# Two stacked recurrent layers on one core: the second layer's input product by Strassen on two levels as well

## The chip, the cores and the metric

The kernel runs on one core of a Trainium2 chip. The time is device time in microseconds. The kernel before took 1686.3 us (median of three runs, 1686.29 to 1686.43).

## What is computed

The input `x` holds 128 sequences of 128 time steps with 512 features, all in float32. Layer 0 is a gated recurrence, layer 1 a plain one, each with a residual connection:

```python
# layer 0, Wh and Wz are the halves of W
gate  = sigmoid(h @ Wh.T + z_t @ Wz.T + b0)
h_new = tanh(h * (1 - alpha) + gate * z_t)
x     = x + hs                       # all steps
# layer 1, on the new x
h_new = tanh(x_t @ Wx + b1 + h @ Wh1)
out   = x + hs
```

Both layers start from the same condition tensor (128 x 512). The products with `h` (the state products) must be made step by step. The products with the inputs (`z @ Wz.T`, `x @ Wx`) can be made for several steps at once.

## The kernel before, in words

**Tiling.** A step's activations lie transposed in SBUF, features on the partitions, as 4 blocks of 128 features by 128 sequences. Steps are taken in groups of `G` = 4; `ring[g]` (tile `T`) holds a group's inputs, and the residuals are added into it. Layer 1 runs `LAG` = 9 steps behind layer 0, so in most steps `t` TensorE makes layer 0's state product of step t, layer 1's of step t - 9, and a share of the input products.

**State products.** Each is 2 halves of 8 matmuls of 128 x 128 x 128 (`state_product`, L332) into the PSUM tiles `r0a`, `r1a` (layer 0) and `r0b`, `r1b` (layer 1). Those tiles are seeded beforehand with the input product: layer 1's by a copy on ScalarE (`seed`, L328), layer 0's by one VectorE addition of two terms (`seed_deep`, L474). Then follow, for layer 0 on each half, the sigmoid on ScalarE (`gate0`, L522), three VectorE operations (`mix0`, L528 and L531), the tanh (`tanh0`, L536), and for layer 1 one tanh (`tanh1`, L551). GpSimd adds each half to the residual (L540).

**Input products.** For a group of 4 steps, the matrix product is split into 2 x 2 blocks and made by Strassen's scheme in 7 products, in the order `OUTER` = 1, 2, 6, 5, 7, 3, 4. Layer 1 (`multiply`, L268) makes each of the 7 by 4 matmuls with 256 columns. Layer 0 (`multiply_deep`, L403) splits each of the 7 again, into 7 matmuls with 128 columns. The activations that Strassen's scheme needs beside the plain blocks are sums: the outer ones (tiles `sa`, `sb`, 512 wide, four per group) are made on GpSimd, layer 0's inner ones (tile `inner`, raw and nested, eight operations of 512) on VectorE, all at L210.

The products of a group accumulate into PSUM: 1, 6, 7 and 4 into one set, 5 and 3 into another, 2 into a third (layer 1) or again the second (layer 0). Between the products of one set the running sum has to be read out. After 1, 6 and 5 ScalarE copies it to SBUF (`keep`, L277; `keep_deep`, L416), after 2, 7 and 3 VectorE adds it to an earlier copy (`add`, L294; `add_deep`, L437), after 4 ScalarE copies it (`last`). A set of layer 0 is two PSUM banks, moved by two operations of 512 and 384 elements. For layer 0 two more VectorE operations on half a group join the inner parts (`gather`, L471 and L472).

**Order.** All operations are put at planned times (`at(time, fn, ...)`) and emitted sorted by time; each engine's queue then runs strictly in that order, and only semaphores make it wait. A step's start is the sum of planned costs: `STATE` for a state product, `PRODUCT` for one of the 7 products of the plain kind, `DEEP` for one of the twice split kind. The shares of a period of four steps are: in the first, layer 1's products 7, 3, 4; in the second, layer 0's 1, 2, 6, 5; in the third, layer 0's 7, 3, 4; in the fourth, layer 1's 1, 2, 6, 5. Steps with 3 and with 4 products thus alternate. In the last group and after it (t >= 125) layer 1 runs with fewer products per step, and at the end alone.

Of the kernel before, what the change touches and what calls it, by code (L numbers as in the profile page):

```python
# [13 lines left out]
def kernel(  # L14
# [37 lines left out]
    P = 128  # L52
# [17 lines left out]
    work = ctx.enter_context(tc.tile_pool(name="work", bufs=2))  # L70
# [8 lines left out]
    STATE, PRODUCT, DEEP = 3.57, 1.73, 1.56  # L79
    OUTER = 1, 2, 6, 5, 7, 3, 4  # L80
# [24 lines left out]
    for t in range(T + LAG + 4):  # L105
        start.append(clock)
        layers = (t < T) + (t >= LAG)
        busy = STATE * layers + (STATE + 0.6 if t < G - 1 else 0.0)
        for layer, g, which in shares(t):
            busy += (DEEP if layer == 0 and g > 1 else PRODUCT) * len(which)  # L110
        clock += max(busy, STATE + (3.0 if t < T else 0.7))
# [39 lines left out]
    cond_in = work.tile([P, C, P], F32, tag="s", name="cond_in")  # L151
    condT = const.tile([P, C, P], F32, tag="condT", name="condT")

    def load_small():
        nc.gpsimd.memset(rows, 0.0)
        for i, v in enumerate((b0, alpha, b1)):
            nc.gpsimd.dma_start(
                out=rows[: Q * C, i], in_=v.rearrange("(a j) -> a j", j=S)
            )
        cond_view = cond.rearrange("(a i) (q r) -> q i a r", i=S, q=Q)  # L160
        for q in range(Q):
            nc.gpsimd.dma_start(out=cond_in[q * S : (q + 1) * S], in_=cond_view[q])

# [36 lines left out]
    COMBINATION = {5: 0, 6: 1, 7: 2, 4: 3}  # L200

    def sums(eng, out, a, which):
# [3 lines left out]
            6: (lambda: out(0), lambda: a(0, 0), ALU.subtract),  # L206
            7: (lambda: a(0, 0), lambda: a(1, 0), ALU.subtract),
            3: (lambda: a(0, 1), lambda: out(1), ALU.subtract),
        }[which]
        eng.tensor_tensor(out(SUM[which]), one(), two(), op)  # L210
# [11 lines left out]
    banks = {}  # L222

    def bank(tag, name):
        banks[tag] = psum.tile([P, 4, P], F32, tag=tag, name=f"{tag}_{name}")

    class Layer:

        X, V, V2 = "B0", "B1", "A1"

        def __init__(self, name):
            self.name = name
            self.S, self.kept, self.pre, self.state = {}, {}, {}, {}
            self.w = const.tile([P, C, C, P], F32, tag=f"w{name}", name=f"w{name}")
            self.wh = const.tile([P, C, C, P], F32, tag=f"wh{name}", name=f"wh{name}")
            self.wc = const.tile([P, 4, 2, 2, P], F32, tag=f"wc{name}", name=f"wc{name}")

# [5 lines left out]

        def act(self, g, i, k):
# [3 lines left out]
        def add_up(self, g, which):  # L248
            if which == 5:
                self.S[g] = spool.tile(  # L250
                    [P, 4, 2, H, P], F32, tag=f"s{self.name}", name=f"s{self.name}_{g}"
                )
            sums(nc.gpsimd, lambda j: self.S[g][:, j], lambda i, k: self.act(g, i, k), which)

        def left(self, g, i):
            return self.S[g][:, SUM[i]] if i in SUM else self.act(g, *PAIRS["left"][i])

        def right(self, i):
            return self.wc[:, COMBINATION[i]] if i in COMBINATION else self.block(*PAIRS["right"][i])

        def multiply(self, g, i, tag, first):
            if first:
                bank(tag, f"{self.name}_{g}_{i}")
            ps = banks[tag].rearrange("p (m h) b -> p m (h b)", m=2)
            a, w = self.left(g, i), self.right(i)
            for m in range(2):
                for c in range(2):
                    nc.tensor.matmul(  # L268
                        ps[:, m], w[:, c, m, :], a[:, c],
                        start=first and m == 0 and c == 0, stop=c == 1, skip_group_check=True,  # L270
                    )

        def evacuate(self, dst, tag, half):

            for m in range(2):
                f = 2 * half + m
                nc.scalar.activation(  # L277
                    dst[:, 2 * m : 2 * m + 2], banks[tag][:, 2 * m : 2 * m + 2], AF.Identity,
                    bias=per_feature[:, 2, f : f + 1],
                )  # L280

        def keep(self, g, i, tag, half):
            s = spool.tile([P, 4, P], F32, tag=f"k{self.name}_{i}", name=f"k{self.name}_{g}_{i}")
            self.evacuate(s, tag, half)
            self.kept[i] = s

        def result(self, g, i, half):
            self.pre[g, i, half] = cpool.tile(
                [P, 4, P], F32, tag=f"c{self.name}_{i}{half}", name=f"c{self.name}_{g}_{i}{half}"
            )  # L290
            return self.pre[g, i, half]

        def add(self, g, i, half, tag, kept):
            nc.vector.tensor_tensor(self.result(g, i, half), banks[tag], self.kept[kept], ALU.add)  # L294

        def last(self, g, tag):
            self.evacuate(self.result(g, 1, 0), tag, 0)

        def products(self, g, which, time):

            X, V, V2 = self.X, self.V, self.V2
            plan_of = {
                1: (X, True, self.keep, (g, "p1", X, 0)),
                5: (V, True, self.keep, (g, "p5", V, 1)),
                6: (X, False, self.keep, (g, "u2", X, 1)),
                3: (V, False, self.add, (g, 0, 1, V, "u2")),
                7: (X, False, self.add, (g, 1, 1, X, "p5")),
                2: (V2, True, self.add, (g, 0, 0, V2, "p1")),
                4: (X, False, self.last, (g, X)),
            }  # L310
            for i in which:
                tag, first, fn, args = plan_of[i]
                at(time, self.multiply, g, i, tag, first)
                time += PRODUCT
# [3 lines left out]
        def from_inputs(self, t, half):  # L318
            g, k = divmod(t, G)
            return self.pre[g, k // H, half][:, k % H :: H]  # L320
# [7 lines left out]
        def seed(self, t, half):  # L328

            nc.scalar.copy(self.state_bank(t, half), self.from_inputs(t, half))  # L330
# [10 lines left out]

    INNER = 1, 2, 6, 3, 7, 4, 5

    class DeepLayer(Layer):

        X, V, V2 = "A0", "B0", "B0"

        def __init__(self, name):
            super().__init__(name)
            self.wi = const.tile([P, 2, 4, 4, P], F32, tag=f"wi{name}", name=f"wi{name}")  # L350
            self.inner, self.parts = {}, {}

        def combine_inner(self, kind, which, eng):

            out = self.wi[:, kind]
            if kind == 0:
                w = self.w.rearrange("p (k a) (n b) f -> p a b k n f", a=2, b=2)
                out = out.rearrange("p (k n) j f -> p j k n f", k=2)
                combinations(eng, lambda j: out[:, j], lambda a, b: w[:, a, b], which)
            else:  # L360
                combinations(eng, lambda j: out[:, :, j], lambda a, b: self.wc[:, :, a, b], which)

        def add_up_inner(self, g, kind, which, eng):
            if kind == 0 and which == 5:
                self.inner[g] = spool.tile([P, 2, 4, 4, P], F32, tag="inner", name=f"inner_{g}")
            out = self.inner[g][:, kind]
            if kind == 0:
                x = ring[g].rearrange("p (k a) (i b) n -> p b a i k n", a=2, b=2)
                out = out.rearrange("p (i k) j n -> p j i k n", i=2)
                sums(eng, lambda j: out[:, j], lambda b, a: x[:, b, a], which)  # L370
            else:
                sums(eng, lambda j: out[:, :, j], lambda b, a: self.S[g][:, :, a, b], which)

        def left_inner(self, g, outer, i):
            if outer in SUM:
# [321 lines left out]
```

## Time and profile before

| | before |
|---|---|
| median of 3 runs | 1686.3 us |
| the profiled execution | 1686.1 us |
| its span | 1684.3 us (1.8 us lie around it) |
| granted TensorE clock | 0.999 |
| busy: TensorE, VectorE, ScalarE, GpSimd | 1662.6, 1036.1, 687.8, 798.3 us |
| one period of four steps | 51.62 us |

The span is what the profile's times count from. "PE" is TensorE, "PEld" its weight loads, "DVE" VectorE, "ACT" ScalarE, "POOL" GpSimd, "SP" the queue that issues most DMAs. A matmul in float32 stands as two records, so 4 matmuls are "x8" and 7 are "x14". A matmul's recorded end lies some 0.16 us behind the start of the next one, as they are pipelined; the time that a matmul costs is therefore read from start to start. One core runs, so there is one row of everything.

The period is read off the starts of layer 1's products: 407.77 and 459.39 us, and so on through the span.

### The profile page before, as it was taken

Reading aid. Unit: us, or ns where it says so; the run is one execution under the profiler, and the core shown is the slowest. Engines: PE = TensorE matmul, PEld = TensorE weight load, DVE = VectorE, ACT = ScalarE, POOL = GpSimd, SP = SyncE. Lnnn points to the kernel's source line nnn. Section 1 sums busy time; section 2 is a strip of 40 time slices with the busy share of each in tenths; the row PEclk is TensorE's granted clock in tenths of the full one; section 3 lists DMA queues with packets and bytes.
Section 4 is the critical chain, followed back from the end, with each engine's and each line's share of the span. In section 5 each row is a group of like instructions: output and inputs, shape, how many; then the busy total and the mean of one; then the engine's idle time right before and its main releaser. Section 6 shows DMA issues by size and latency. Waiting matters only on the chain.

```text
span 1684.3 us, 33340 instructions
## 1 busy us (share of the span) xinstructions
PE 1662.6 (99%) x13108; PEld 1611.2 (96%) x13108; DVE 1036.1 (62%) x1924; ACT 687.8 (41%) x1796; POOL 798.3 (47%) x788
## 2 busy tenths in 40 slices
PE   6999999999999999999999999999999999999998
PEld 6999999999999999999999999999999999999998
DVE  4676666666566665666666666656666666666431
ACT  1544344444344433444434444344444344444343
POOL 3754445544444554355444445543554444554333
PEclk9999999999999999999999999999999999999999
DMA  8101211121121112111211111112111111110112
GB/s 173 53 14 41 46 41 39 40 50 39 39 46 44 39 39 45 44 39 39 48 42 39 43 42 43 38 42 48 38 39 44 45 39 38 44 46 20 20 32 51
DMA packets 153212, 73.76 MB, mean 44 GB/s; under 512 B 16800, under 2 KB 151968, under 8 KB 153056
## 3 DMA queue, kind: packets, MB, share of 16 engines
q1 hardware_dynamic: 148992, 69.53, 18.5%
q10 hardware_dynamic: 3840, 1.84, 0.6%
q8 instruction: 103, 1.69, 0.4%
q14 instruction: 53, 0.43, 0.1%
q0 software_dynamic: 224, 0.27, 0.1%
HBM read 38.02 MB, written 33.55 MB: 42 GB/s over the span
## 4 chain that ended last, share of the span: by engine, by line
PE 95%; DMA 2%; DVE 1%; ACT 1%; issue 0%; SPq 0%; POOLq 0%; POOL 0%; DVEq 0%; ACTq 0%
PE B_b L268 20%; PE r0b L337 14%; PE r1b L337 13%; PE r0a L337 13%; PE r1a L337 13%; PE A_a L403 11%; PE B_a L403 8%; PE A_b L268 3%; DMA x<-in_x_dram 1%; DVE s L531 0%; DMA wh_in<-in_L_cond_W_dram 0%; DMA wz_in<-in_L_cond_W_dram 0%; PE r1a L493 0%; SPq L122 0%; PE B_a L268 0%
## 5 line engine op out<-in xcount | busy, mean ns | idle before, releaser
L540 POOL TENSOR_TENSOR T<-T,h 128x256 f32<-128x256 f32 x512 | 429.8, 851 | 758.5 <-ACT h L536 726.0
L337 PE MATMUL r0a<-h,wha 128*128 128x128 f32 x2032 | 248.5, 275 | 1.1 <-ACT h L536 1.1
L337 PE MATMUL r0b<-h,whb 128*128 128x128 f32 x2032 | 248.4, 275 | 0.1
L337 PE MATMUL r1b<-h,whb 128*128 128x128 f32 x2032 | 247.7, 275 | 0.0
L337 PE MATMUL r1a<-h,wha 128*128 128x128 f32 x2032 | 247.6, 275 | 0.0
L337 PEld LDWEIGHTS r0a<-h,wha 128*128 128x128 f32 x2032 | 242.2, 192 | 5.1 <-ACT h L536 1.7
L337 PEld LDWEIGHTS r0b<-h,whb 128*128 128x128 f32 x2032 | 237.8, 192 | 1.0 <-ACT h L551 0.7
L337 PEld LDWEIGHTS r1a<-h,wha 128*128 128x128 f32 x2032 | 237.1, 192 | 0.0
L337 PEld LDWEIGHTS r1b<-h,whb 128*128 128x128 f32 x2032 | 237.1, 192 | 0.0
L536 ACT ACTIVATE h<-s 128x256 f32<-128x256 f32 x256 | 106.7, 417 | 305.4 <-DVE s L531 305.4
L528 DVE TENSOR_TENSOR r0a<-r0a,T 128x256 f32<-128x256 f32 x128 | 54.9, 429 | 250.6 <-ACT r0a L522 250.6
L268 PE MATMUL B_b<-sb,wcb 128*128 128x256 f32 x768 | 176.3, 379 | 0.0
L268 PEld LDWEIGHTS B_b<-sb,wcb 128*128 128x128 f32 x768 | 143.3, 190 | 18.1
L522 ACT ACTIVATE r0a<-r0a,per_feature 128x128 f32<-128x128 f32 x256 | 87.6, 342 | 154.8 <-PE r0a L337 150.6
L210 POOL TENSOR_TENSOR sa<-T 128x512 f32<-128x512 f32 x62 | 93.0, 1500 | 119.5 <-DVE T L174 119.5
L403 PE MATMUL A_a<-inner,wia 128*128 128x128 f32 x720 | 139.2, 275 | 0.0
L179 DVE STREAM_TRANSPOSE o<-T 128x512 f32<-128x512 f32 x128 | 90.1, 704 | 36.9 <-POOL T L540 33.6
L528 DVE TENSOR_TENSOR r1a<-r1a,T 128x256 f32<-128x256 f32 x128 | 55.3, 432 | 91.0 <-ACT r1a L522 91.0
L403 PEld LDWEIGHTS A_a<-inner,wia 128*128 128x128 f32 x720 | 109.3, 192 | 0.0
L403 PE MATMUL B_a<-inner,wia 128*128 128x128 f32 x540 | 104.4, 275 | 0.0
L210 DVE TENSOR_TENSOR inner<-sa 128x512 f32<-128x512 f32 x60 | 86.0, 1434 | 23.3 <-POOL sa L210 23.3
L174 DVE STREAM_TRANSPOSE T<-x 128x512 f32<-128x512 f32 x128 | 86.8, 681 | 13.1 <-DMA x<-in_x_dram 12.1
(137 smaller groups left out, 2628.6 us busy)
## 6 DMA issues: line engine op xcount, KB each, us to landing
out_dram<-o SPq DMA_DIRECT2D x510, 64.0 KB, 1.8
x<-in_x_dram SPq DMA_DIRECT2D x502, 64.0 KB, 2.5
wx_in<-in_L_cond_Wx_dram SPq DMA_DIRECT2D x4, 256.0 KB, 7.0
wh_in<-in_L_cond_Wh_dram SPq DMA_DIRECT2D x4, 256.0 KB, 9.5
x<-in_x_dram ACTq DMA_DIRECT2D x10, 64.0 KB, 4.0
wz_in<-in_L_cond_W_dram ACTq DMA_DIRECT2D x2, 256.0 KB, 6.2
wz_in<-in_L_cond_W_dram SPq DMA_DIRECT2D x2, 256.0 KB, 5.6
wh_in<-in_L_cond_W_dram ACTq DMA_DIRECT2D x2, 256.0 KB, 6.0
```

The source lines that it names most:

```text
L174: nc.vector.transpose(dst.rearrange("p c (a i) -> p c a i", i=S), src.rearrange("p a (c j) -> p c a j", j=S))
L179: nc.vector.transpose(dst.rearrange("p a (c j) -> p c a j", j=S), src.rearrange("p c (a i) -> p c a i", i=S))
L210: eng.tensor_tensor(out(SUM[which]), one(), two(), op)
L268: nc.tensor.matmul(ps[:, m], w[:, c, m, :], a[:, c], start=first and m == 0 and c == 0, stop=c == 1, skip_group_check=True,)
L337: nc.tensor.matmul(ps[:, m], self.wh[:, c, 2 * half + m, :], h[t - 1][:, c], start=alone and m == 0 and c == 0, stop=c == C - 1, skip_grou ...
L403: nc.tensor.matmul(banks[f"{tag}{part}"][:, place], self.right_inner(outer, i), self.left_inner(g, outer, i), start=first and place == 0, ...
L522: nc.scalar.activation(gate[:, m], gate[:, m], AF.Sigmoid, bias=per_feature[:, 0, f : f + 1])
L528: nc.vector.tensor_tensor(gate, gate, at_of(t)[:, two[i]], ALU.mult)
L536: nc.scalar.activation(h0[t][:, two[i]], s0[t][:, two[i]], AF.Tanh)
L540: nc.gpsimd.tensor_tensor(r, r, h[t][:, two[i]], ALU.add)
```

## The change

Layer 1 is given the same class as layer 0. Each of its 7 products becomes 7 matmuls of 128 columns, with its own inner weight combinations (`raw`, `nested`) and inner sums of activations. Only layer 0's group 1 keeps the plain products. With that:

- **PSUM sets.** There are two sets of two banks, `A` and `B`. A set is one tile of 8 places, of which 7 are used, and is moved by one operation of 896 elements (`keep`, `add`, `last`) in place of two of 512 and 384 (layer 0) or of 512 or twice 256 (layer 1). Layer 0 accumulates 1, 6, 7, 4 in A and 2, 5, 3 in B; layer 1 the other way round.
- **Sums.** The raw sums are made for three of the four blocks only, the nested ones for two pairs; they become VectorE operations of 256 (`R12`, `N56`, `N73`) and 128 elements (`R4`), 16 per group and layer. All sums lie in tiles that both layers share by turns (`buffer`). `sum_up` lays down when they are made.
- **Seeds.** Both layers' state tiles are seeded by a ScalarE copy (`seed`) and a VectorE addition in place (`seed_second`).
- **Bias and residual.** Layer 1's bias moves from the copies to the tanh, which becomes two operations of 128 elements per half. The residual is one GpSimd operation of 512 elements in place of two of 256.
- **Times.** `finish` (the transposition and the stores of the output) and `prepare_x` move from 0.6 and 0.7 us after a step's start to 6.35 and 6.4 us. At the start, 16 matmuls on a zeroed tile are put ahead of everything (`warm_up`), and several preparations move between engines and steps.

```diff
+    def cost(layer, g):
+        return PRODUCT if (layer, g) == ("a", 1) else DEEP
...
+    def warm_up():
+        ps = [L1.state_bank(-1, half) for half in range(2)]
+        for n in range(16):
+            nc.tensor.matmul(
+                ps[n % 2].rearrange("p m b -> p (m b)"), condT[:, 0], condT[:, 0:2].rearrange("p c b -> p (c b)"),
+                start=True, stop=True,
+            )
...
+        def add_up_raw(self, g, row, which, eng):
+            x = ring[g].rearrange("p (k a) (i b) n -> p b a i k n", a=2, b=2)
+            if row == 0:
+                out = buffer((self.name, g), "R12", [P, 2, 4, P])
+                sums(eng, lambda j: out[:, :, SUM[j]], lambda b, a: x[:, b, a, 0], which)
+            else:
+                out = buffer((self.name, g), "R4", [P, 4, P])
+                sums(eng, lambda j: out[:, SUM[j]], lambda b, a: x[:, b, a, 1, 1], which)
+
+        def add_up_nested(self, g, pair, which, eng):
+            S = shared[(self.name, g), "S" + pair]
+            out = buffer((self.name, g), "N" + pair, [P, 2, 4, P])
+            sums(eng, lambda j: out[:, :, SUM[j]], lambda b, a: S[:, :, a, b], which)
...
         def multiply(self, g, outer, tag, first):
+            if first:
+                sets[tag] = psum.tile([P, 8, P], F32, tag=tag, name=f"{tag}_{self.name}_{g}_{outer}")
...
+            for n, i in enumerate(INNER):
+                nc.tensor.matmul(
+                    sets[tag][:, n], self.right(outer, i), self.left(g, outer, i),
+                    start=first and n % 4 == 0, stop=True, skip_group_check=True,
+                )
...
+        def keep(self, g, i, tag):
+            self.kept[i] = spool.tile([P, 7, P], F32, tag=f"k_{i}", name=f"k{self.name}_{g}_{i}")
+            n = self.places(g)
+            nc.scalar.copy(self.kept[i][:, n], sets[tag][:, n])
...
         def add(self, g, i, half, tag, kept):
+            n = self.places(g)
+            nc.vector.tensor_tensor(self.part(g, i, half)[:, n], sets[tag][:, n], self.kept[kept][:, n], ALU.add)
...
         def seed(self, t, half):
-            nc.scalar.copy(self.state_bank(t, half), self.from_inputs(t, half))
+            nc.scalar.copy(self.state_bank(t, half), self.terms(t, half)[0])
+
+        def seed_second(self, t, half):
+            for term in self.terms(t, half)[1:]:
+                ps = self.state[t, half]
+                nc.vector.tensor_tensor(ps, ps, term, ALU.add)
...
-    L0, L1 = DeepLayer("a"), Layer("b")
+    L0, L1 = Layer("a", "A", "B"), Layer("b", "B", "A")
...
-    def residual(t, i, h):
-        r = at_of(t)[:, two[i]]
-        nc.gpsimd.tensor_tensor(r, r, h[t][:, two[i]], ALU.add)
+    def residual(t, h):
+        nc.gpsimd.tensor_tensor(at_of(t), at_of(t), h[t], ALU.add)
...
     def tanh1(t, i):
...
-        nc.scalar.activation(h1[t][:, two[i]], ps, AF.Tanh)
+        for m in range(2):
+            f = 2 * i + m
+            nc.scalar.activation(h1[t][:, f], ps[:, m], AF.Tanh, bias=per_feature[:, 2, f : f + 1])
...
-        at(start[3] + 0.1 + 0.4 * kc, permute_w1, L1.w, "wx", kc)
+        at(start[1] + 2.5 + 0.1 * kc, permute_w1, L1.w, "wx", kc)
...
+    def sum_up(layer, g, outer, b, c):
+        for n, i in enumerate((5, 6, 3, 7)):
+            at(outer[n // 2] + 0.1 * n, layer.add_up, g, i, nc.gpsimd)
+            at(b + 0.1 + 0.01 * n, layer.add_up_raw, g, 0, i, nc.vector)
+            at(b + (3.3, 3.31, 5.1, 5.11)[n], layer.add_up_nested, g, "56", i, nc.vector)
+            at(c + 0.1 + 0.01 * n, layer.add_up_nested, g, "73", i, nc.vector)
+            at(c + (3.3, 3.31, 5.1, 5.11)[n], layer.add_up_raw, g, 1, i, nc.vector)
...
-                    at(end + 0.5 if (u + 1) % G else due, L1.seed, u + 1, i)
-                at(end + 0.6, residual, u, i, h1)
-            at(start[t + 1] + 0.6 if u + 1 < T else end + 1.4, finish, u)
+                    if (u + 1) % G:
+                        copy, add = end + 0.6, end + 1.05
+                    else:
+                        copy, add = (start[t + 1] + x if t + 1 < T else start[t + 1] - 0.02 for x in (0.05, 1.4))
+                    at(copy, L1.seed, u + 1, i)
+                    at(add, L1.seed_second, u + 1, i)
+            at(end + 0.7, residual, u, h1)
+            at(start[t + 1] + 6.35 if t + 1 < T else end + 1.4, finish, u)
...
+        if k == 1 and 0 <= g - 2 < NG:
+            at(start[t] - (0.9 if t < T else 0.03), L1.gather, g - 2, 0, nc.vector)
+            at(start[t] + 1.0 if t >= T else start[t + 1] - 0.9, L1.gather, g - 2, 1, nc.vector)
+        if k == 0 and 3 <= g + 1 < NG:
+            sum_up(L0, g + 1, (start[t] + 9.0, start[t + 1] + 9.0), start[t + 1], start[t + 2])
+        if k == 2 and 1 <= g - 1 < NG - 2:
+            sum_up(L1, g - 1, (start[t] + 9.0, start[t + 1] + 9.0), start[t + 1], start[t + 2])
```

## The prediction, made before the changed kernel ran

> **What bounds the kernel now.** First the page's busy times, then the windows (name of the stretch, its length, busy time of PE, PEld, DVE, ACT, POOL with instructions, granted clock, DMA share, GB/s):
>
> ```profile
> PE 1662.6 (99%) x13108; PEld 1611.2 (96%) x13108; DVE 1036.1 (62%) x1924; ACT 687.8 (41%) x1796; POOL 798.3 (47%) x788
> ...
> 160.00:1600.00 1440.00, 1440.00 (x11436) 1399.51 (x11435) 915.36 (x1694) 597.53 (x1561) 685.99 (x668) 1.00 0.18 41
> 1640.00:1684.00 44.00, 38.70 (x295) 36.70 (x293) 7.48 (x11) 13.82 (x36) 15.19 (x19) 0.97 0.27 54
> ```
>
> PE has no gap in 160 to 1600 us, at full clock; DVE is busy 64% of that stretch. So a shorter PE stream shortens the kernel until another engine delivers too late. The chain that ended last prices PE's pieces (start, us, what):
>
> ```profile
> 80.30 1.79 PE r1a L337 x16
> 82.09 1.56 PE A_a L403 x14
> 83.65 1.73 PE B_b L268 x8
> ```
>
> A product of layer 1 costs 1.727 us (24 records take 5.18), one of layer 0's twice split kind 1.563 (starts 419.93, 421.50, 423.06), a half state product 1.786. A period is 8 x 3.573 + 7 x 1.727 + 7 x 1.563 = 51.6 us, the period measured.
>
> Who delivers to PE in a step is read off the timeline of one that starts at S = 400.46:
>
> ```profile
> 400.46 1.95 PE L337 MATMUL r0a<-h,wha 128*128 128x128 f32 x16
> 402.45 0.72 ACT L522 ACTIVATE r0a<-r0a,per_feature 128x128 f32<-128x128 f32 x2 [0.95 <-PE r0a L337]
> 403.20 0.43 DVE L528 TENSOR_TENSOR r0a<-r0a,T 128x256 f32<-128x256 f32 x1 [3.29 <-ACT r0a L522]
> 404.36 0.42 ACT L536 ACTIVATE h<-s 128x256 f32<-128x256 f32 x1 [1.20 <-DVE s L531]
> 404.69 0.70 ACT L522 ACTIVATE r1a<-r1a,per_feature 128x128 f32<-128x128 f32 x2
> 405.42 0.43 DVE L528 TENSOR_TENSOR r1a<-r1a,T 128x256 f32<-128x256 f32 x1 [0.68 <-ACT r1a L522]
> 405.88 0.61 DVE L531 SCALAR_TENSOR_TENSOR s<-h,leak,r1a 128x128 f32<-128x128 f32 x2
> ```
>
> DVE begins the second mix at S+4.96 and ends it at S+6.03, whatever the change does in between, since it waits for ACT's second sigmoid. Last the groups by shape, for prices (busy, mean ns, idle before):
>
> ```profile
> L210 DVE TENSOR_TENSOR inner<-inner,sa 128x512 f32<-128x512 f32 x16 | 10.9, 683 | 0.0
> L210 DVE TENSOR_TENSOR inner<-T,inner 128x512 f32<-128x512 f32 x16 | 17.6, 1101 | 0.6
> L472 DVE TENSOR_TENSOR ca<-ca 128x256 f32<-128x256 f32 x30 | 18.9, 629 | 1.0
> L437 DVE TENSOR_TENSOR ca<-B_a,ka_u 128x512 f32<-128x512 f32 x15 | 10.4, 692 | 5.1 <-PE B_a L403 5.1
> L437 DVE TENSOR_TENSOR ca<-B_a,ka_u 128x384 f32<-128x384 f32 x15 | 8.4, 558 | 0.0
> ```
>
> One kind of sum takes 0.68 or 1.10 us: the long ones lie beside a running POOL operation. L472 is likewise two operations in one, 0.42 at 437.98 with POOL idle and 0.83 at 445.15 beside it. Additions that read PSUM (L437) take 0.69 in both cases.
>
> **Part 1, the products.** Each of 32 groups saves 7 x (1.727 - 1.563) = 1.15 us of PE: **-36.8**. All of it lies on the path; the new period is 50.47.
>
> **Part 2, DVE.** Prices: 256 elements 0.43, 512 0.69, 128 some 0.30 (from 0.683 and 0.425 by a straight line), 896 from PSUM 0.692 + 384 x (0.692 - 0.558)/128 = 1.09. A period of four steps then holds 8 transpositions 5.5, 8 mixes of 1.07 8.6, 16 second seeds 6.9, 6 additions 6.6, 4 gathers of 1.11 4.5, 24 sums of 256 10.3, 8 sums of 128 2.4: **44.8 us of 50.5**, against some 33.0 before (660.6 in 400 to 1432 us, 20 periods). DVE is not the bound, but its order now matters. I follow it through a period.
>
> The tightest step is the third, layer 0's 7, 3, 4. Product 4 writes into set A, so PE waits there for the addition after product 7. Queued ahead of that on DVE, after the second mix (S+6.03): two R4 sums 0.60, two transpositions 1.37, four second seeds 1.72, the addition 1.09; S+10.81. Successive independent operations overlap by 0.07 (L531 ends 406.49, a seed starts 406.52, the next operation 406.87, before the seed's end): seven times, S+10.3. PE is there at 7.15 + 2 x 1.563 = S+10.27. The fourth seed waits for ACT (last tanh, then copy, at S+8.7); it falls due at 8.75, so that wait is nearly hidden. Stall: 0.05 to 0.1.
>
> In the first step two of the seeds fall after the gather, 0.7 us of slack. Behind it, though, DVE has add, gather, four R12 sums and then layer 1's seeds: add from S+10.45, gather to S+12.9 (one operation beside POOL), R12 to S+14.6, first seed to S+15.0, which is 3.2 us into the next step; PE wants it 3.57 in. Slack 0.4. The mix behind it starts 0.7 late. In steps of four products PE needs the addition after product 2 by S+11.84; product 2 ends at S+10.44, the addition at S+11.55: 0.3. ACT's copy after product 1 (0.585 + 3 x 0.107 = 0.91 us, S+9.3 to S+10.2) must end before product 6 at S+10.27: 0.1.
>
> So every handover fits, some by 0.1 to 0.4. What can break them is a DVE sum beside POOL: +0.41 (L472) to +1.06 (a sum of 683 reached 1.75). By the order, POOL's residual comes after the second mix and its sums after the second residual, while DVE has transpositions and PSUM operations; mainly the gathers (11.5 to 12.9) meet POOL. I take **0.15 us per period, x 29 = +4.4**; between 0 and 0.84 (two handovers late by 0.42).
>
> [...]
>
> **Part 3, ACT and POOL.** ACT per period: 32 halves of gate and tanh of layer 1 at 0.35, 8 tanhs 0.42, 16 copies 0.38, 8 set copies 0.91 = 28 of 50.5, hidden. POOL: 16 operations of 1.27 = 20, hidden; before, 24.7. The stores leave 5.7 us later on SP, behind them only loads that are needed 17 us on: nothing.
>
> **Part 4, the end.** From t = 128 PE waits for layer 1 alone. The tanh as two operations ends 0.70 instead of 0.38 after PE: 4 bare steps, +1.3. Group 31 now needs gather and second seed between its additions and step 124 of layer 1: the addition after product 3 ends 0.3 before PE is done, gather 1.1, copy 0.4, second seed 0.5: +1.8 (before, the copy was done 0.37 early, 1663.08 against 1663.45). One residual of 1.27 for 0.72 at the end: +0.55. One late seed at t = 129: +0.3. Sum **+4.0**.
>
> **Part 5, the start.** PE's first matmuls run at half speed (timeline, records of four):
>
> ```profile
> 13.97 1.06 PE L493 MATMUL r0a<-T,wa 128*128 128x128 f32 x4
> 14.82 1.06 PE L493 MATMUL r1a<-T,wa 128*128 128x128 f32 x4
> 15.68 0.74 PE L493 MATMUL r0a<-T,wa 128*128 128x128 f32 x4
> ...
> 22.89 1.99 PE L268 MATMUL A_a<-sa,wca 128*128 128x256 f32 x8 [1.69 <-POOL sa L210]
> ```
>
> Four records take 0.85 at first and 0.45 from 16.2, with the page's clock at full. The warm-up should make the input product 1.9 us shorter, but two products later PE waits for POOL's sums until 22.89 all the same: 0 on the path. [...] Moved to step 1, layer 1's weight copies on ACT (2.18 us at 56.73) stand ahead of `tanh0`: +1.1; step 3 loses them, -0.3. The inner sums of group 2 left PE idle twice for 0.92 (waits for `h` at 70 and 78 us); their smaller form should return one. Taken as **0**, between -2 and +3.
>
> **Sum.** Against the profiled execution, 1686.1 (0.2 under the median): 1686.1 - 36.8 + 4.4 + 4.0 + 0 = **1657.7**, say 1658.
>
> **Rivals.**
>
> *Handovers late.* In two of four steps a POOL meeting of 0.42 lies ahead of the addition that PE waits for: 0.84 x 29 = 24.4 in place of 4.4: 1678. For it: margins of 0.1 to 0.4, and rows of 1.1 to 1.75. Against: the order puts POOL's work beside PSUM operations.
>
> *DVE becomes the bound: slower.* 40 operations per period (32 sums, 8 halves of gathers) have two SBUF inputs, before 12. At 0.42 for each that meets POOL, DVE passes the old period from (51.6 - 44.8)/0.42 = 17 on. At 24 of 40 the period is 54.9, 3.3 x 29 = 96 more: about 1786. For it: POOL is busy 40% of the time, and the late engine stays late. Against: POOL's 16 operations are fewer than before and come while DVE has other work.
>
> *No stall at all*, a tail of +2: 1686.1 - 36.8 + 2 = 1651, the low end.
>
> **Chances.** Forecast with its 0 to 0.5 us per period (1648 to 1670): 0.60. Handovers late (1670 to 1683): 0.24. Between them and no change: 0.05. DVE the bound: 0.11. A measurement here can tell 0.2%, 3.4 us. Faster 0.84, same 0.05, slower 0.11. Range 1648 to 1682: it leaves out the slow cases, and little at the low end (no stall, no tail, 2 us from the start).
>
> **What would show it.** Right: layer 1's products at 1.563 and periods of 50.5 to 50.7; the wait of PE on DVE's `add` under 5 us in total; PE near 99%. Wrong: L224 sums of 256 at a mean above 0.7 us, PE waiting for seeds (`r0b`) or for `h` each period, or a period over 51.6.

## The result, and the profile after

| | before | after |
|---|---|---|
| median | 1686.4 us (4 runs beside the changed kernel) | 1671.3 us (1667.7 to 1672.0) |
| ratio | | 0.9906, 95% interval 0.9888 to 0.9923 |
| the profiled execution, its span | 1686.1, 1684.3 us | 1672.0, 1670.2 us |
| granted TensorE clock | 0.999 | 0.994 |
| one period of four steps | 51.62 us | 50.48 us |

The changed kernel is faster, by 14 to 15 us and not by the forecast 28. The time lies in the forecast range (1648 to 1682) and its sign is right; half of the gain is missing, and the two profiles say where. First the page's busy times and the windows of the changed kernel (columns as in the prediction):

```profile
PE 1642.3 (98%) x14484; PEld 1633.5 (98%) x14484; DVE 1321.9 (79%) x2976; ACT 793.5 (48%) x2046; POOL 666.0 (40%) x541
```

```profile
0.00:26.00 26.00, 19.49 (x87) 16.29 (x88) 13.56 (x24) 1.87 (x2) 10.77 (x18) 0.93 0.87 163
26.00:40.00 14.00, 13.76 (x83) 12.26 (x83) 6.29 (x15) 4.55 (x9) 5.41 (x5) 0.89 0.74 192
...
160.00:1600.00 1440.00, 1438.38 (x12879) 1438.08 (x12878) 1177.86 (x2676) 707.31 (x1830) 571.30 (x454) 1.00 0.18 42
1600.00:1640.00 40.00, 34.49 (x287) 34.10 (x286) 22.28 (x43) 14.47 (x39) 12.76 (x10) 0.91 0.20 40
1640.00:1670.00 30.00, 21.60 (x169) 20.84 (x167) 10.13 (x18) 9.69 (x29) 6.33 (x5) 0.90 0.22 45
```

Through the long middle PE is as full as before (1438.4 of 1440 us) at full clock, though DVE went from 915 to 1178 us. Both ends have a granted clock of 0.89 to 0.93 (the kernel before had 1.00 from 26 to 40 and from 1600 to 1640 us) and, at the back, a PE that stands: 34.5 of 40 us busy. PE's longest waits name the places (us in total, times, longest):

```profile
PE r0b L435 <- DVE r0b L428: 8.1, 3, 4.8
PE A_a L343 <- POOL S_a L224: 3.3, 1, 3.3
PE B_b L349 <- DVE cb L373: 3.0, 3, 1.6
```

A ledger makes this exact. For each step the start of its state product on PE is read from the timeline, and the one of the changed kernel is subtracted from that of the kernel before: what has been gained up to there, in us of the profiled executions (u counts layer 1's steps).

| up to | after | e_first_group | e_finish | e_plain1 | e_best |
|---|---|---|---|---|---|
| layer 0, t = 0 | -2.46 | -2.52 | -0.91 | -1.31 | -0.69 |
| t = 2 | -3.31 | -2.77 | -1.76 | -2.16 | -0.93 |
| t = 6 | -2.12 | -2.47 | -0.57 | -0.97 | -0.61 |
| t = 11 | -6.01 | -4.75 | -4.44 | -0.37 | -2.03 |
| t = 13 | -4.86 | -3.60 | -3.30 | -0.37 | -0.89 |
| t = 117 | 24.68 | 25.95 | 26.25 | -0.37 | 28.66 |
| t = 124 | 26.48 | 27.74 | 28.05 | -0.37 | 30.46 |
| t = 125 | 25.08 | 26.36 | 26.65 | -0.37 | 30.79 |
| layer 1, u = 118 | 25.73 | 27.01 | 27.30 | -0.37 | 31.44 |
| u = 120 | 20.45 | 21.72 | 27.81 | -0.62 | 32.09 |
| u = 123 | 18.80 | 19.45 | 25.46 | -0.62 | 31.17 |
| u = 125 | 14.90 | 15.57 | 24.23 | -0.62 | 33.04 |
| end of the span | 14.1 | 14.8 | 23.5 | -1.4 | 32.2 |

From t = 13 to 117 the gain is 29.54 us in 26 periods, 1.136 per period against 1.15 forecast. So the products pay what was promised. Measured against the 1.15 us that each of layer 1's groups was to bring, some 7 us are lost before t = 11, 1.9 around step 124 and some 13 after layer 0's end. My theory was: the start loses to a fallen clock and to sums that come late for layer 1's first group, the end to the order on DVE. The rival: the new work on DVE is too much everywhere, and whatever is moved only changes the place of the wait.

### The profile page after: what moved, and what is told of

Same layout as the page of the kernel before. It is cut to its first block, busy times and chain, and to the rows that moved or that the text cites. A ratio compares the mean times of both kernels' runs of the same rounds, so it can differ in the third digit from the quotient of the medians.

```text
span 1670.2 us, 37100 instructions
## 1 busy us (share of the span) xinstructions
PE 1642.3 (98%) x14484; PEld 1633.5 (98%) x14484; DVE 1321.9 (79%) x2976; ACT 793.5 (48%) x2046; POOL 666.0 (40%) x541
## 4 chain that ended last, share of the span: by engine, by line
PE 90%; DVE 3%; issue 3%; POOL 2%; ACT 1%; DMA 1%; POOLq 0%; ACTq 0%; DVEq 0%; SPq 0%
PE r0a L435 13%; PE r0b L435 13%; PE r1b L435 13%; PE r1a L435 12%; PE A_a L349 11%; PE B_b L349 11%; PE A_b L349 8%; PE B_a L349 8%; POOL T L493 1%; DMA x<-in_x_dram 1%; DVE h L485 1%; PE A_a L343 0%; DVE cb L373 0%; DVE N_b L224 0%; POOL S_a L224 0%
## 5 line engine op out<-in xcount | busy, mean ns | idle before, releaser
L493 POOL TENSOR_TENSOR T<-T,h 128x512 f32<-128x512 f32 x256 | 326.6, 1276 | 973.6 <-ACT h L490 890.2
L490 ACT ACTIVATE h<-h 128x256 f32<-128x256 f32 x256 | 106.7, 417 | 276.7 <-DVE h L485 273.9
L435 PEld LDWEIGHTS r0a<-h,wha 128*128 128x128 f32 x2032 | 237.3, 192 | 0.7 <-ACT h L490 0.6
L476 ACT ACTIVATE r1a<-r1a,per_feature 128x128 f32<-128x128 f32 x256 | 85.3, 333 | 4.2
L502 ACT ACTIVATE h<-r0b,per_feature 128x128 f32<-128x128 f32 x256 | 78.1, 355 | 16.6 <-PE r0b L435 16.6
L224 POOL TENSOR_TENSOR S_a<-T 128x512 f32<-128x512 f32 x62 | 79.8, 1287 | 14.6 <-DVE T L187 14.6
L502 ACT ACTIVATE h<-r1b,per_feature 128x128 f32<-128x128 f32 x256 | 80.8, 371 | 10.1 <-PE r1b L435 8.0
L224 POOL TENSOR_TENSOR S_b<-T 128x512 f32<-128x512 f32 x64 | 81.8, 1278 | 1.5 <-issue 1.5
L485 DVE SCALAR_TENSOR_TENSOR h<-h,leak,r0a 128x128 f32<-128x128 f32 x254 | 77.0, 345 | 5.3
L485 DVE SCALAR_TENSOR_TENSOR h<-h,leak,r1a 128x128 f32<-128x128 f32 x254 | 77.1, 345 | 4.5
```

The source lines that it names most:

```text
L224: eng.tensor_tensor(out(which), one(), two(), op)
L435: nc.tensor.matmul(ps[:, m], self.wh[:, c, 2 * half + m, :], h[t - 1][:, c], start=alone and m == 0 and c == 0, stop=c == C - 1, skip_grou ...
L476: nc.scalar.activation(gate[:, m], gate[:, m], AF.Sigmoid, bias=per_feature[:, 0, f : f + 1])
L485: nc.vector.scalar_tensor_tensor(h0[t][:, f], h0[t - 1][:, f], leak[:, f : f + 1], gate[:, m], ALU.mult, ALU.add)
L490: nc.scalar.activation(h0[t][:, two[i]], h0[t][:, two[i]], AF.Tanh)
L493: nc.gpsimd.tensor_tensor(at_of(t), at_of(t), h[t], ALU.add)
```

## The start: what the warm-up did

PE's rows of the changed kernel at the start (the timeline; start, us, what, and in brackets the idle time before and who ended it):

```profile
17.87 1.89 PE L343 MATMUL B_a<-T,wa 128*128 128x256 f32 x8
23.07 3.78 PE L343 MATMUL A_a<-S_a,wca 128*128 128x256 f32 x8 [3.31 <-POOL S_a L224]
26.64 3.04 PE L343 MATMUL B_a<-S_a,wca 128*128 128x256 f32 x8
29.52 1.89 PE L343 MATMUL A_a<-S_a,wca 128*128 128x256 f32 x8
```

The warm-up did shorten the input product, from 5.5 to 4.2 us. PE then came earlier to the same wait for POOL's sums, stood 3.31 us in place of 1.69, and the two products behind the gap took 3.57 and 2.88 us instead of 2.34 and 1.83. Two runs tell the parts apart.

**Without the warm-up.** In `warm_up`, 2 products in place of 16:

```diff
-        for n in range(16):
+        for n in range(2):
```

> The changed kernel with 2 warm-up products in place of 16. Theory: the warm-up costs the start. It shortens the input product, but the sums on POOL are not earlier, so PE stands for 3.31 us before product 6 (1.69 in the kernel before), and the two products behind that gap took 3.57 and 2.88 us in place of 1.73. Without it the gap is again some 1.7 us, both products take 1.73, and layer 0's first state product starts near 30.5 us in place of 32.97: 2.5 us faster than the changed kernel's 1671.3. Rival: PE's first matmuls at half speed are on the path and the warm-up saves their 1.9 us: 1.9 us slower, first state product near 35.

Measured: 1669.3 us (0.9898, 0.9883 to 0.9912). The gap is 1.81 us, the products behind it take 2.34 and 1.83 us as in the kernel before, and layer 0 starts at 31.14 in place of 32.97 us: 1.8 better, not 2.5, since in this run PE had POOL's sums only at 23.52 us, 0.63 later than in the kernel before. The rival's 1.9 us to the other side is excluded.

**With the gap filled.** Seven products of 256 columns, used by nobody, between product 2 and product 6:

```diff
+    def fill():
+        ps = [L1.state_bank(-2, half) for half in range(2)]
+        for n in range(7):
+            nc.tensor.matmul(
+                ps[n % 2].rearrange("p m b -> p (m b)"), L0.w[:, 0, 0], L0.w[:, 0, 0:2].rearrange("p m f -> p (m f)"),
+                start=True, stop=True,
+            )
...
+    at(19.12, fill)
```

> The changed kernel with seven more products of 256 columns, whose result nobody uses, between product 2 and product 6 of layer 0's first group, where PE stands for 3.31 us. Theory: it is the standing itself that brings the granted clock down; with PE busy for about 3.0 of the 3.3 us, products 6 and 5 take 1.73 us each and the first state product starts near 30.0 to 30.5 us in place of 32.97: 2.5 to 3 us faster than the changed kernel. Rival: the granted clock falls because PE began early and has worked a fixed time; then products 6 and 5 stay at 3.6 and 2.9 us, and the time is the changed kernel's.

Measured: 1668.6 us (0.9896, 0.9881 to 0.9911). The same rows:

```profile
22.38 0.59 PE L181 MATMUL r0b_-2_227<-wa 128*128 128x256 f32 x2
22.89 1.99 PE L352 MATMUL A_a<-S_a,wca 128*128 128x256 f32 x8
25.23 1.99 PE L352 MATMUL B_a<-S_a,wca 128*128 128x256 f32 x8 [0.35 <-DVE ca L382]
```

PE has no gap, product 6 is at full speed, and layer 0 starts at 30.51 us, to 0.01 where it started before the change. Of the 2.46 us, 2.28 are the two products behind the longer standing (6.45 us against 4.17), and 0.18 that POOL's sum was ready later in the changed kernel (PE went on at 23.07, here at 22.89). Beginning early had nothing to do with it. The medians of these runs and of the next (1668.6 to 1670.4) lie within the spread of the changed kernel's own (1667.7 to 1672.0): the rows decide here, not the times.

## Layer 1's first group

**Copies and raw sums moved.** The raw sums one step earlier; ACT's copies of layer 1's weights (2.17 us, from 43.52) behind step 1's second tanh:

```diff
-        at(start[1] + 2.5 + 0.1 * kc, permute_w1, L1.w, "wx", kc)
+        at(start[1] + 5.4 + 0.1 * kc, permute_w1, L1.w, "wx", kc)
-        at(start[1] + 3.0 + n, L1.combine_weights, i, nc.gpsimd)
+        at(start[1] + 5.8 + 0.01 * n, L1.combine_weights, i, nc.gpsimd)
-        at(start[6] + (2.6, 2.61, 4.4, 4.41)[n] - 0.2, L1.add_up_raw, 0, 0, i, nc.vector)
+        at(start[5] + 0.1 + 0.01 * n, L1.add_up_raw, 0, 0, i, nc.vector)
```

> The changed kernel with two things moved at the start: the raw sums of layer 1's first group one step earlier on DVE (PE waited 1.85 us for them within that group's first product), and ACT's copies of layer 1's weights from ahead of step 1's first tanh to behind its second (with POOL's sums of these weights behind them). Theory: the changed kernel loses some 7 us in its first eleven steps, about 1.85 of it to the late raw sums and 0.85 to the copies: 2 to 2.7 us faster than the changed kernel at step 11. Rival: DVE is full there and whatever is moved makes the next thing late (additions after product 7, first seeds): under 0.7 us.

Measured: 1670.4 us (0.9905, 0.9890 to 0.9920), and by the ledger 1.26 us at t = 11, between the two. The copies gave 0.60 (t = 0 to 2). PE's wait for the raw sums is gone (1.6 us better from t = 6 to 7), but their four operations, each 0.57 to 0.95 us beside POOL, now make step 5's mix late, and 0.9 is lost there (t = 2 to 6). Here the rival is half right.

## The steady part: how near the edge it is

The prediction's narrowest handover, the addition after product 7 in the third step, in the changed kernel (timeline; this step starts at 425.34):

```profile
433.94 0.42 DVE L428 TENSOR_TENSOR r1b<-r1b,cb 128x256 f32<-128x256 f32 x1
...
434.27 1.08 DVE L373 TENSOR_TENSOR ca<-A_a,ka_p 128x896 f32<-128x896 f32 x1
...
435.61 0.50 PE L349 MATMUL A_a<-T,wca 128*128 128x128 f32 x3
```

The addition ends at 435.35 and PE goes on at 435.61 without a gap. To see whether these 0.26 us are all there is, one instruction that nobody needs was put ahead of that addition in 27 periods:

```diff
+    def extra():
+        nc.vector.tensor_tensor(spare, condT[:, 0:2], condT[:, 2:4], ALU.add)
...
+        if k == 2 and 3 <= g < NG - 2:
+            at(start[t] + 8.74, extra)
... e_extra_2: twice; e_extra_turn: in place of the sum
+        nc.vector.transpose(spare.rearrange("p c (a i) -> p c a i", i=S), condT[:, 0:2].rearrange("p c (a i) -> p c a i", i=S))
```

> The changed kernel with one sum of 256 elements more on DVE in 27 periods (0.42 us by the trace), right ahead of the addition after product 7 of layer 0, the tightest handover. Its result is not used. Theory: in the changed kernel that addition ended 0.26 us before PE needed it; 0.34 to 0.42 more leaves 0.08 to 0.16 us of PE idle, 27 times: 2 to 4.5 us more by the last step of layer 0, with PE's periods going from 50.48 to 50.6. Rival A (as forecast: no margin): 0.34 to 0.42 times 27, 9 to 11 us. Rival B (DVE has 18% of its time free and makes it good elsewhere): nothing.

> The same with two such sums in each of the 27 periods. Theory (margin 0.26): 0.42 to 0.58 us each time, 11 to 16 us more. Rival A (no margin): 18 to 23. Rival B (slack elsewhere): nothing. Between this run and the one with one sum the step is a whole sum, 0.34 to 0.42 us per period, if the margin is used up by the first.

> The changed kernel with one more DVE operation of the same size at the same place as the extra sum, but a transposition, which has one input (0.35 us, half of the 0.70 that one of 512 elements takes). Theory: the extra sum cost 0.64 us per period because it has two inputs in SBUF and took 0.81 us beside POOL's sum, not because DVE had 0.42 us more to do; a transposition there keeps its 0.35 us, of which the margin of 0.26 takes most: 0 to 0.1 us per period, 0 to 3 us in all. Rival: what counts is one more instruction in a full queue (and the restart of PE after each wait): 0.3 to 0.6 us per period, 8 to 16 us, as with the sum.

Measured: 1687.6 us with one sum (1.0002, 0.9993 to 1.0012: the whole gain of the change is gone), 1726.0 with two (1.0235, 1.0220 to 1.0251), 1673.4 with the transposition (0.9924, 0.9910 to 0.9937). No theory had the sums right. The transposition cost 0.24 us per period, between the theory (0 to 0.1) and the rival (0.3 to 0.6); its time rose by 2 us only, but not as the theory had it: part of the ledger's 6.1 us was made good by a start that lost nothing (t = 0 at +0.12, where the changed kernel lost 2.46). The mean pitches in that step, from the start of one product on PE to the next:

| | addition later by | product 3 | product 4 | PE's loss per period | t = 13 to 117 by the ledger |
|---|---|---|---|---|---|
| after | | 1.566 | 1.567 | | |
| one transposition | 0.33 | 1.704 | 1.665 | 0.24 | 6.1 |
| one sum | 0.73 | 2.109 | 1.665 | 0.64 | 16.7 |
| two sums | 2.14 | 3.516 | 1.703 | 2.1 | 54.9 |

In each row, what the addition is late by, less what product 3 grows by, is the margin: 0.19 us each time. So the margin is 0.2 (the 0.26 of the trace less some 0.06 to hand over), and each stall costs a further 0.10 to 0.14 in the product behind it (1.665 and 1.703 against 1.567). The surprise is the size of the sums. DVE and POOL in the runs with one and with two (each sum is 0.42 us elsewhere):

```profile
435.67 1.27 POOL L498 TENSOR_TENSOR T<-T,h 128x512 f32<-128x512 f32 x1 [0.37 <-ACT h L507]
...
436.41 0.81 DVE L180 TENSOR_TENSOR spare<-condT 128x256 f32<-128x256 f32 x1
...
436.90 1.46 POOL L229 TENSOR_TENSOR S_b<-T 128x512 f32<-128x512 f32 x1
...
437.14 1.08 DVE L378 TENSOR_TENSOR ca<-A_a,ka_p 128x896 f32<-128x896 f32 x1
```

```profile
442.37 1.27 POOL L498 TENSOR_TENSOR T<-T,h 128x512 f32<-128x512 f32 x1 [0.36 <-ACT h L507]
...
443.11 2.22 DVE L180 TENSOR_TENSOR spare<-condT 128x256 f32<-128x256 f32 x2
...
443.60 1.45 POOL L229 TENSOR_TENSOR S_b<-T 128x512 f32<-128x512 f32 x1
```

The one sum comes while POOL's residual runs and ends at 437.22, 0.28 after that ends at 436.94. POOL's next sum, issued meanwhile, takes 1.46 in place of 1.27. With two, the second sum ends at 445.33, again 0.28 after POOL's sum ends at 445.05. In these rows the two engines take turns, instruction by instruction. The transposition, with one input, took 0.43 us in all 27 places; the one at 432.83 ran while POOL was at a residual (432.10 to 433.37).

## The second level undone

Layer 1 by one level again (`e_plain1`): every place that names layer 0's group 1 as plain now names layer 1 too, and layer 1's raw and nested sums, its nested weights and its gathers go.

```diff
-            if (self.name, g) == ("a", 1):
+            if (self.name == "b" or g == 1):
```

> The changed kernel with layer 1's products by Strassen on one level again (8 matmuls of 256 columns in place of 14 records of 128), without layer 1's inner sums and gathers; warm-up, sets of two banks and shared tiles stay. Theory: the second level is worth its full 1.15 us in each of layer 1's 32 groups while PE is the bound, and costs what was lost in the first layer-1 group (some 3.5 us in steps 7 to 10), in step 124 (1.9) and in the last ten steps (some 12): so the period is again 51.62, and the time lands near 1671.3 + 36.8 - 17 = 1691, with 2.5 to 3.3 us of the loss at the start still there: slower than the kernel before by 2 to 6 us. Rival: the losses at the end come from the other parts (sets of two banks, the tanh in two operations) and stay: 1700 to 1708.

Measured: 1687.4 us (1.0007, 0.9997 to 1.0016). The period is the old one to the last digit (the ledger stands at -0.37 from t = 9 to 127), DVE is at 829 us in the window from 160 to 1600, the start loses 0.4 us and the end 1.0. So everything else in the change (sets of two banks, shared tiles, the tanh in two operations, one residual operation) costs 1.4 us in all, and what is lost from t = 6 to 11, at t = 124 and behind layer 0's end comes with layer 1's second level: its sums, gathers and second seeds. It came out 4 us lower than expected, mostly because the start lost 0.4 us and not 2.5 to 3.3.

## The end: one instruction that waits at the head of a queue

DVE, PE and POOL in the changed kernel where PE stands longest (timeline):

```profile
1612.73 1.26 POOL L493 TENSOR_TENSOR T<-T,h 128x512 f32<-128x512 f32 x1 [5.33 <-ACT h L502]
...
1614.02 0.71 DVE L192 STREAM_TRANSPOSE o<-T 128x512 f32<-128x512 f32 x1 [4.12 <-POOL T L493]
1614.66 0.83 DVE L224 TENSOR_TENSOR N_b<-S_b,N_b 128x256 f32<-128x256 f32 x1
1615.41 1.75 DVE L402 TENSOR_TENSOR cb<-cb 128x512 f32<-128x512 f32 x1
...
1617.87 0.42 DVE L428 TENSOR_TENSOR r0b<-r0b,cb 128x256 f32<-128x256 f32 x1
...
1618.35 3.79 PE L435 MATMUL r0b<-h,whb 128*128 128x128 f32 x16 [4.80 <-DVE r0b L428]
```

From t = 127 on `finish` is planned 1.4 us behind the step's second half, before POOL has done that step's residual. DVE stands 4.12 us at its transposition, with the gather and the seeds that PE needs behind it; the gather then meets POOL's sums and takes 1.75 us for 0.69. PE stands 4.80 us, and its next half product takes 3.58 us for 1.79. The same happens at u = 124 (2.32 us, then 3.52).

**The transposition moved**, and with it (in the run named e_tail) group 30's gather ahead of the sums. In e_tail the last step's transposition came ahead of its residual, so that addition is not in that kernel's last step and its end is some 2.2 us shorter than e_finish's (by the ledger from u = 127 on); its time is too good by that much.

```diff
-            at(start[t + 1] + 6.35 if t + 1 < T else end + 1.4, finish, u)
+            at(start[t + 1] + 6.35 if t + 1 < T else start[t + 1] + 2.0 if u + 1 < T else end + 1.4, finish, u)
... e_tail only:
-            at(start[t] - (0.9 if t < T else 0.03), L1.gather, g - 2, 0, nc.vector)
+            at(start[T] + 0.2 if t == T + 1 else start[t] - (0.9 if t < T else 0.03), L1.gather, g - 2, 0, nc.vector)
```

> The changed kernel with another order on DVE in the last ten steps: the transposition of a finished step stands behind the next additions and seeds (it waits 3 to 4 us for POOL's residual), and group 30's gather ahead of the sums that wait for POOL. Theory: of the 25.7 us gained by step 127, some 11 are lost behind it in two waits of PE for a seed (4.80 and 2.32 us) and in the low clock after each (2.3 and 1.7 us). The 4.8 us wait goes with its low clock, the 2.3 us one shrinks to about 1.5: 8 to 10 us faster than the changed kernel, about 1662. Rival: what bounds these steps is the chain of tanh, additions, gather and seeds that each step needs (longer since the change), and the order in DVE's queue hardly matters: under 2 us.

> The changed kernel with one move: from the end of layer 0 on, DVE's transposition of a finished step stands some 2 us into the next step, behind that step's additions, gather and seeds (the last step keeps its place). The gather of group 30 stays where it was. Theory: this instruction, which waits 3 to 4 us for POOL's residual with everything else of DVE's queue behind it, makes about half of what the tail loses; the rest is the gather that meets POOL, which stays: 4 to 7 us faster than the changed kernel, PE's longest wait for a seed (4.80 us) down to 1 to 3. Rival: the wait for POOL only fills time in which DVE has nothing to do; the late sums and gather make the loss: under 1.5 us.

Measured: e_tail 1662.3 us (0.9855, 0.9839 to 0.9871), e_finish 1663.8 us (0.9867, 0.9852 to 0.9882). From u = 119 to 127 the changed kernel loses 10.4 us, e_finish 3.6: 6.8 won, and the step from u = 119 to 120 loses nothing. The gather's move adds nothing to that (e_tail loses 5.2 there). The rival falls.

## All of it together

`e_best` takes the filler, the two moves at the start, and further: the nested sums of layer 1's first group in one go, its block of raw sums for product 4 ahead of step 8's second mix, its first seeds between the next group's raw sums; the nested sums for step 126 planned in step 125, not 124, and the sums behind them a step later too; the last steps' transpositions 3.0 us into the next step; their gathers where both inputs are ready (the first 0.2 us into a step); and the last group's products as below.

```diff
-(OUTER[0:1], OUTER[1:2], OUTER[2:3], OUTER[3:5], OUTER[5:])
+(OUTER[0:1], OUTER[1:2], OUTER[2:4], OUTER[4:6], OUTER[6:])
...
-                    if (u + 1) % G:
+                    if (u + 1) % G or t >= T:
...
-        at(start[7] + (2.6, 2.61, 4.4, 4.41)[n], L1.add_up_nested, 0, "56", i, nc.vector)
+        at(start[7] + 2.6 + 0.01 * n, L1.add_up_nested, 0, "56", i, nc.vector)
...
-                at(start[t + 1] + 1.4, L1.seed_second, 0, i)
+                at(start[t + 1] + 0.115, L1.seed_second, 0, i)
```

> The changed kernel with its losses taken one by one: seven products nobody uses in PE's gap at the start; layer 1's weight copies behind step 1's second tanh; raw and inner sums of layer 1's first group earlier, its first seeds ahead of half of the next group's raw sums; inner sums for step 126 spread over steps 124 and 125; the last steps with the transpositions of finished steps behind the seeds, gathers where both inputs are ready, and the last group's products as 1, 1, 2, 2, 1 per step in place of 1, 1, 1, 2, 2. Theory: the ledger of the changed kernel adds up, so the losses come back: about 2 us from the clock, 3 to 4 from the other items at the start, 1.5 to 1.9 in step 124, 8 to 10 in the last ten steps: 1654 to 1657, some 30 us under the kernel before. Rival: part of them are one chain seen twice, and what is moved makes the next thing late: 1659 to 1664, no better than the run with the transposition alone moved.

Measured: **1653.7 us** (1653.3 to 1653.9; ratio to the kernel before 0.9807, 0.9794 to 0.9820), 17.5 us under the changed kernel's median and 10 under e_finish: the low edge of the theory (1654 to 1657), far from the rival (1659 to 1664). In its window from 1600 to 1640 us PE has no gap:

```profile
1600.00:1640.00 40.00, 40.00 (x355) 39.75 (x354) 27.88 (x49) 18.54 (x47) 13.65 (x11) 1.00 0.22 43
```

By the ledger the steps from u = 118 to 127 now win 1.6 us where the changed kernel lost 10.9, step 124 wins 0.3 where it lost 1.4, and t = 0 to 11 loses 1.3 where it lost 3.6. Which of the further moves gave how much within these stretches was not told apart.

## Why the prediction was right, and where it was not

The sign and the steady part were foreseen. That the time lies in the range is partly luck: 1671.3 us lies above the forecast's own stretch (1648 to 1670, chance 0.60) and in that of the rival "Handovers late" (1670 to 1683, 0.24), whose 0.84 us per period did not come. Losses of 22.3 us at the start, in step 124 and at the end, which the sum had at 4.0, put it there.

**Part 1, the products: right.** 1.136 us per period in the steady part, and none of it in e_plain1, whose ledger stands still there.

**Part 2, DVE: right in kind, too dear by 4 us.** What is missing of the gain is 0.014 us per period, not 0.15 (0.4 us in place of 4.4). The addition after product 7 ended at S+10.01, not at S+10.3, because more of the short operations overlap than I let: the two sums of 128 took 0.20 each, not 0.30, and the four seeds 0.33 each. PE's arrival, S+10.27, was right. The gathers meet POOL as said (1.13 and 0.98 us mean for 0.69), with slack behind them.

**What a meeting costs.** I had priced a sum of 256 beside POOL at +0.41. In the runs with the extra sums 0.42 became 0.81 or about 1.4, in the rows shown ending 0.28 us behind POOL's instruction. The profiles of both kernels between 40 and 1650 us show the same: of DVE's additions of 256 and 512 elements from SBUF to SBUF, every lengthened one (over 0.44 and 0.70 us), 180 before and 132 after, ended 0.28 (256) or 0.55 us (512), to within 0.01, behind an instruction of POOL. So the +0.41 was read off meetings in which little of POOL's instruction was left. What spared the kernel is where the meetings fall, not that they are cheap.

**The rival "DVE the bound"** had the mechanism that the extra sums show. It needed 17 of a period's 40 operations to be lengthened; in the changed kernel's steady part 4 were, the first halves of the gathers, and the L224 sums of 256 kept a mean of 0.42 us. One sum with two inputs ahead of the tight addition, while POOL works, is enough to undo the change (e_extra_1).

**Part 4, the end: the step that failed.** I priced +4.0; it cost 13.2, and step 124 1.9 more. I listed the new work (tanh, gather and seed, residual), whose tanh in two operations cost nothing (the last bare steps take 3.88 us against 3.87). I did not follow `finish` past the end of layer 0, where its plan time changes from 6.35 us into a step to 1.4 us behind the state product, ahead of the seeds that had become DVE's. And I had no term for PE's clock after standing.

**Part 5, the start: the other step that failed.** Taken as 0, between -2 and +3, it was 7.2 us. I saw that the warm-up moved PE's wait and did not shorten it, and called that nothing; with the longer wait layer 0 began 2.46 late. The copies ahead of `tanh0` cost 0.6 to 0.85 of the 1.1 I gave them. Layer 1's first group, some 5 us by the ledger with its own gain of 1.15 not arriving, was not in the sum at all: I had costed the sums of a period and not those of the first group, which come while POOL still combines weights. Between t = 2 and 6 some 1.2 us came back, where the sum had hoped for one.

**The sum.** 1686.1 - 36.8 + 0.4 (steady) + 1.9 + 13.2 (step 124 and the end) + 7.2 (start) = 1672.0, the profiled execution. The forecast had + 4.4 + 4.0 + 0. The rival of late handovers (1678) was nearer in the number and wrong in the place.

## What to carry to other kernels

Here a saving per period arrived almost whole in the steady part, and half of it was lost at the ends: cost the first and the last group on their own, with every instruction that waits at the head of an in-order queue. Whether there is slack is measured by an instruction that nobody needs, put ahead of the tight handover; one that itself waits for another engine (here the sum) measures that wait as well, so take one that does not (here the transposition). And an engine that is made to arrive earlier at a wait it cannot move may come out of it slower (here 6.45 us in place of 4.17 for the two products behind the wait).

## What was not expected of the hardware

**TensorE's clock fell after 2.32 us of standing already.** Standings of PE behind the start's input product, from timelines and lists of waits, and what followed. At full clock the first product behind the start's gap has 1.99 us on record (before, e_no_warm, e_fill), a half state product 1.95:

| PE stood | where | what followed |
|---|---|---|
| 1.62 us | after, step 124 | the product behind it 1.67 us from start to start, as behind shorter waits; mean clock 1.00 from 160 to 1600 us |
| 1.69 and 1.81 us | before and e_no_warm, start | products of 1.99 and 1.99 us in both, clock 1.00 |
| 1.8 us in the mean, 2.1 at most | e_extra_2, 27 periods | the product behind it 1.703 us in the mean, against 1.665 behind the shorter waits of e_extra_1; mean clock 1.00 from 160 to 1600 us |
| 2.32 us | after, u = 124 | a half state product of 3.68 us |
| 2.78 us | e_finish, start | products of 2.93 and 2.69 us |
| 2.8 us | e_extra_turn, start | nothing lost by the ledger (+0.12 at t = 0) |
| 3.17 us | e_tail, start | products of 3.59 and 1.89 us |
| 3.20 us | e_extra_1, start | products of 2.95 and 2.66 us |
| 3.31 us | after and e_first_group, start | products of 3.78 and 3.04, 3.78 and 3.00 us |
| 4.80 us | after, end | a half state product of 3.79 us |

In these cases up to 1.81 us cost nothing, from 3.17 on what followed was slower each time, and between them it was the one or the other. The granted clock shows more. The changed kernel's start, cut where the clock changes (windows):

```profile
18.72:22.13 3.41, 1.04 (x5) 0.57 (x3) 3.41 (x5) 0.00 (x0) 2.31 (x2) 1.00 1.18 189
22.13:28.96 6.83, 5.89 (x14) 4.72 (x15) 5.03 (x7) 0.59 (x1) 6.67 (x6) 0.50 0.55 129
28.96:32.37 3.41, 3.41 (x18) 3.00 (x17) 0.69 (x1) 1.87 (x2) 2.00 (x2) 1.00 0.38 99
```

In this trace the clock falls to a half for 6.83 us from 22.13 and from 1616.16, for 3.41 us from 1646.88, and once more behind PE's last matmul, at 1667.36; its seven changes lie whole multiples of 3.413 us apart. Cut the traces of the kernel before and of the changed one into stretches of that length at the changes: PE stood for 2.32 us or more in each of the five stretches ahead of a fall (2.37, 2.60, 2.32 and, behind the last matmuls, 2.85 and 3.41), and for 1.56 at most in every other one at full clock that began behind its first matmul. The clock came back after stretches in which PE did not stand, and not after those with 0.94 and 2.2 us. If it is the same in the other runs, a wait of 2 to 3 us leaves the clock full where one of these times cuts it in two, and 2.8 us can cost nothing in e_extra_turn and 2.78 something in e_finish; that is my estimate from these two traces, and no run was made to show it. It would also explain why runs of one kernel differ by 4 us here (1667.7 us at a mean clock of 0.998, the others 1670.9 to 1672.0 at 0.994 and 0.995), and those of e_best, whose longest wait behind the start's input product is 0.7 us, by 0.6.

**Sums on DVE and POOL took turns.** The DVE sums with two inputs in SBUF that POOL lengthened ended 0.28 us (256 elements) after POOL's instruction. The gather of 512 elements at 1615.41, above, ended at 1617.16, 0.55 after POOL's sum of 1615.16 ended at 1616.61. With one input in SBUF (a transposition) or a PSUM input the time stayed as it was: in the kernel before, transpositions took 0.67 to 0.71 us with and without POOL beside them, additions of 512 from PSUM 0.68 or 0.69.
